# Moving tile loads and stores from ScalarE's queue to GpSimd's in an attention and expert kernel

## The chip, the cores and the metric

The kernel runs on one core of a Trainium2 chip. A core has five engines, each with its own instruction stream that it works off in order: TensorE (PE in the profile; PEld is its weight load), VectorE (DVE), ScalarE (ACT), GpSimd (POOL) and SyncE (SP). An engine that reaches an instruction whose input isn't there waits, and all that stands behind it waits too. Transfers between memory and the core's buffers are carried by 16 DMA engines, but an instruction on one of the engines' streams starts each of them. The metric is the device time of one launch in microseconds; the time before is the median of three runs, 1396.2 us (1394.3 to 1397.18).

## What is computed

The input is x of shape (8, 1024, 256), float32: 8192 rows of 256. The output adds two branches to x, both fed with the layer norm of x:

```
xn  = (x - mean) / sqrt(var + 1e-5)
out = x + attention(xn) + experts(xn)

# attention: 16 heads of 16, causal, linear
q, k = elu(xn Wq^T) + 1, elu(xn Wk^T) + 1;   v = xn Wv^T
kv, ks = cumsum over rows of (k outer v), of k
attention = (q . kv / max(q . ks, 1e-6)) Wo^T

# experts: 8 experts, the two best of each row
logits = xn Wr + br;  two largest, softmax over the two -> weights c
experts = sum over the two of c_e * (silu(xn W1_e) * (xn W3_e)) W2_e
```

W1 and W3 are 256 x 512 per expert, W2 is 512 x 256. Which rows go to which expert is known only while the kernel runs.

## The kernel before

**Tiles.** The rows are cut into 16 tiles of 512 rows (index t, four chunks of 128). A tile's raw rows are `xb`. Four steps make it ready: `moments(t, n)` finds mean and variance (L272) and, for tiles after the fifth, the inverse square root by Newton steps on VectorE (L281 to L291), and writes the factors of the normalisation into the table `tab` (L294 is the last step); `normalise(t)` scales the rows, on ScalarE from tile 4 on (L307); `turn(t)` transposes them on TensorE (L322), copies the result `xnT` out on ScalarE (L327) and stores it to memory as `xnT_d[t]` (L331), from where attention reads it much later; `logits_turned(t)` and `add_logits` compute the router's logits (L340, L345, L361, L351). Every four tiles `route` finds the two best experts of their rows and counts the rows per expert (`both` L413, `run` L421, `cnt_ps` L427 on TensorE).

**Experts.** The rows chosen for an expert are put together in expert tiles of 128 rows (index j), 135 at most. The first 25 come from the first four tiles of x, whose routing is done at the start, in `first_batch()`; the rest are listed when all 16 tiles are routed. For expert tile j: `ffn_load` has GpSimd gather the rows `xg` (L1085) and their `entry` (L1090: weight and the two factors of the norm); `ffn_weights` reads the expert's number `te_i` (L1112) on SyncE and starts the two loads of its W1 and W3 (L1122, 512 KB each); `ffn_norm` scales the rows (L1097, ScalarE); `ffn_turn` transposes them (L1106, copy L1108); `ffn_hidden` makes the gate and up products (`gu_ps` L1139, silu L1147, `hT` L1150); `ffn_out` the second product (`y_ps` L1158) and `y` (L1165, VectorE); `ffn_store` has GpSimd scatter-add y to memory (L1169), for the first 25 into `acc_d`, later into the output.

**The loops.** A start section, whose order is written out by hand, readies tiles 0 to 4, routes 0 to 3 and lists the first 25 expert tiles. Then SyncE issues the loads of W2, tile 6, the copy of x into `acc_d` and the store of the table (L1060), which the entries are gathered from. The main loop (L1208 on) runs over j. In each of its first eleven steps after j = 0 it also readies tile t = 4 + j: every second step the moments of two tiles, then normalise, turn, and the load of tile t + 5 into one of five buffers, then logits and every fourth tile the routing. At j = 0 the loads of tiles 7, 8 and 9 are issued. Interleaved with this the attention of the tiles goes on in small steps, among them two `reciprocal` instructions of 128x512 per tile (L843, their input `den` L842), the masked scores (`s_sb` L872) and the add of the result to memory from GpSimd (L936, L938). `ffn_step(j)` gathers for j + 3, loads weights for j + 2, turns j + 1 and finishes j − 1.

**What sets the order.** Outside the start section the order of the instructions on each engine is not the order of the source: a planner chooses it when the program is built, from priorities and costs of its own; `in_order` and `issue_after` hold some of it. A change in the source can therefore change the order on engines that it doesn't touch. [...]

## Time and profile before

| | |
|---|---|
| median of the three runs | 1396.2 us (1394.3 to 1397.18) |
| profiled execution | 1388.92 us; its span is 1387.1 us, 1.8 us lie around it |
| granted TensorE clock | 0.99 |
| TensorE | 1328.5 us busy, 96% of the span |
| VectorE, ScalarE, GpSimd | 52%, 35%, 38% |
| loads of xb on ScalarE's queue | 9 of 512 KB, 6.0 us from issue to landing (median) |
| stores of xnT on ScalarE's queue | 15 of 512 KB, 4.7 us |
| main loop from the first expert product (53.4 us) to the last prepared tile (about 165 us) | 111.6 us, TensorE 106.5 us busy |

The profile is of one execution, 7.3 us under the median of the runs, so a sum from its rows is a difference to be added to the median. The columns of a timeline row are its start and duration in microseconds, the engine (a q behind it marks the engine's DMA issue), the line of the kernel, the operation, output and inputs with their sizes, how many instructions are taken together, and in brackets the engine's idle time before it and what ended that. A row of waits names the waiting engine and line, what it waited for, and the sum, number and longest of the waits in us. A row of DMA issues gives the issuing queue, number, size and time from issue to landing in us. A busy share is an average; in the tile loop the shares differ from those of the whole.

### The profile page before, as it was taken

How to read it: one execution, taken by the hardware profiler on the slowest of the kernel's cores; microseconds unless marked ns; L12 is line 12 of the kernel's file. 1: busy time of each engine (PE TensorE's matmuls, PEld its weight loads, DVE VectorE, ACT ScalarE, POOL GpSimd, SP SyncE). 2: the span in 40 equal slices, each digit the busy share in tenths (PEclk: the TensorE clock that was granted, in tenths of full speed). 3: DMA queues.
4: the chain of work that ended last, by engine and by line, in shares of the span. 5: the costliest groups of instructions: out<-in, count | busy, mean ns of one | idle time of the engine just before them, and what ended most of it. 6: DMA issues, size and time to landing. Idle time of an engine off the chain costs nothing.

```text
span 1387.1 us, 27907 instructions
## 1 busy us (share of the span) xinstructions
PE 1328.5 (96%) x10906; PEld 1127.2 (81%) x10906; DVE 728.0 (52%) x1428; ACT 488.7 (35%) x914; POOL 528.3 (38%) x457
## 2 busy tenths in 40 slices
PE   5799999999999999999999999999999999999996
PEld 4578887878888888888888888888788788888895
DVE  7786589784353536354453536363544435363631
ACT  5466351141514233252525142342524151423321
POOL 3533332223334333434433333443434244334432
PEclk9999999999999999999999999999999999999999
DMA  9687653455756555555656555565647375555553
GB/s 346 236 275 234 180 169 109 120 143 145 211 160 152 164 124 145 150 145 151 152 147 164 147 151 152 140 173 139 162 129 175 109 173 160 132 164 138 147 151 80
DMA packets 129412, 223.56 MB, mean 161 GB/s; under 512 B 14818, under 2 KB 53346, under 8 KB 128994
## 3 DMA queue, kind: packets, MB, share of 16 engines
q1 hardware_dynamic: 84306, 165.95, 36.9%
q0 software_dynamic: 38064, 43.22, 19.3%
q10 hardware_dynamic: 6912, 12.58, 2.5%
q8 instruction: 90, 1.47, 0.4%
q14 instruction: 40, 0.33, 0.1%
HBM read 187.91 MB, written 44.29 MB: 167 GB/s over the span
## 4 chain that ended last, share of the span: by engine, by line
PE 82%; DVE 11%; ACT 3%; issue 2%; DMA 2%; POOL 0%; POOLq 0%; ACTq 0%; DVEq 0%
PE gu_ps L1139 32%; PE y_ps L1158 15%; PE s_ps L865 6%; PE o_ps L906 4%; PE a_ps L928 4%; PE zq L764 4%; PE zkk L780 3%; PE zkv L780 3%; PE kv_ps L880 2%; DVE rden L843 2%; PE xg_t L1106 2%; PE held_ps L696 2%; PE o_ps L899 2%; PE den L842 2%; DVE ksum L832 2%
## 5 line engine op out<-in xcount | busy, mean ns | idle before, releaser
L1139 PEld LDWEIGHTS gu_ps<-xgT,w 128*128 128x128 f32 x4224 | 494.7, 193 | 28.8 <-issue 17.2
L1139 PE MATMUL gu_ps<-xgT,w 128*128 128x128 f32 x4224 | 511.6, 278 | 2.3 <-DVE s_sb L872 1.9
L1085 POOL DMA_INDIRECT xg<-in_x_dram,src_i x132 | 129.8, 983 | 547.7 <-ACT xgT L1108 437.8
L1158 PE MATMUL y_ps<-w_sb,hT 128*128 x1056 | 251.9, 380 | 2.5 <-DVE hT L1150 1.3
L1169 POOL DMA_INDIRECT out_dram<-y,dst_i x107 | 173.6, 1622 | 159.4 <-DVE y L1165 85.1
L1150 DVE TENSOR_TENSOR hT<-gu_ps,hT 128x512 f32<-128x512 f32 x132 | 90.4, 685 | 248.2 <-PE gu_ps L1139 229.2
L1147 ACT ACTIVATE hT<-gu_ps 128x512 f32<-128x512 f32 x132 | 78.8, 597 | 381.1 <-PE gu_ps L1139 380.2
L1158 PEld LDWEIGHTS y_ps<-w_sb,hT 128*128 128x128 f32 x1056 | 190.0, 190 | 25.9 <-issue 2.6
L872 DVE TENSOR_TENSOR s_sb<-s_ps,causal 128x512 f32<-128x512 f32 x256 | 163.2, 683 | 73.6 <-PE s_ps L865 71.8
L1165 DVE TENSOR_SCALAR y<-y_ps,entry 128x256 f32<-128x256 f32 x132 | 63.7, 482 | 137.6 <-PE y_ps L1158 137.6
L1090 POOL DMA_INDIRECT entry<-tab_d,of_i x107 | 111.2, 1040 | 37.8 <-issue 31.7
L865 PE MATMUL s_ps<-qm,kT 32*128 32x256 f32 x1024 | 107.6, 412 | 3.4 <-DVE rden L843 2.0
L843 DVE RECIPROCAL rden<-den 128x512 f32<-128x512 f32 x32 | 105.4, 3329 | 3.4 <-PE den L842 3.4
L1108 ACT COPY xgT<-xg_t 128x256 f32<-128x256 f32 x132 | 49.0, 372 | 152.3 <-PE xg_t L1106 150.7
L865 PEld LDWEIGHTS s_ps<-qm,kT 32*128 32x128 f32 x1024 | 61.6, 185 | 39.1 <-issue 19.5
L933 ACT COPY at<-a_ps 128x256 f32<-128x256 f32 x64 | 23.8, 372 | 176.9 <-PE a_ps L928 176.7
L1097 ACT ACTIVATE xg<-xg,entry 128x256 f32<-128x256 f32 x132 | 79.6, 603 | 5.6 <-issue 5.6
L928 PE MATMUL a_ps<-wo_sb,oT 128*128 128x256 f32 x256 | 67.2, 384 | 5.7 <-DVE oT L914 5.6
L906 PE MATMUL o_ps<-s_sb,va 128*32 128x128 f32 x2048 | 71.8, 278 | 0.0
L764 PE MATMUL zq<-xnT,wq_sb 128*128 128x512 f32 x128 | 61.0, 609 | 0.0
L928 PEld LDWEIGHTS a_ps<-wo_sb,oT 128*128 128x128 f32 x256 | 47.0, 190 | 16.6 <-DVE oT L914 9.4
L1169 POOL DMA_INDIRECT acc_d<-y,src_i x25 | 44.0, 1761 | 42.2 <-DVE y L1165 30.7
(199 smaller groups left out, 1440.6 us busy)
## 6 DMA issues: line engine op xcount, KB each, us to landing
w<-in_w_dram SPq DMA_DIRECT2D x264, 512.0 KB, 4.4
xnT_d<-xnT ACTq DMA_DIRECT2D x15, 512.0 KB, 4.7
xnT<-xnT_d SPq DMA_DIRECT2D x15, 512.0 KB, 5.9
out_dram<-in_x_dram SPq DMA_DIRECT2D x12, 512.0 KB, 5.2
out_dram<-at POOLq DMA_DIRECT2D x12, 512.0 KB, 7.7
xb<-in_x_dram ACTq DMA_DIRECT2D x9, 512.0 KB, 6.0
w_sb<-in_w_dram SPq DMA_DIRECT2D x4, 1024.0 KB, 11.8
xb<-in_x_dram SPq DMA_DIRECT2D x7, 512.0 KB, 7.4
```

The source lines that it names most:

```text
L764: nc.tensor.matmul(z, lhsT=wq_sb[:, k, bass.ts(o, P)], rhs=xnTs[t][:, k, :], start=(k == 0), stop=(k == KC - 1),)
L843: nc.vector.reciprocal(rden[:, o, :], den)
L865: nc.tensor.matmul(s_ps[r][:, hh].rearrange("p a l -> p (a l)"), lhsT=kT[rows, hh, span], rhs=qm[rows, hh, :, span], start=True, stop=True,)
L872: nc.vector.tensor_tensor(sm, s_ps[r].rearrange("p k a l -> p (k a) l"), causal_b, ALU.mult)
L906: nc.tensor.matmul(o_ps[32 * r : 32 * r + 32, hh, :], lhsT=va[:, c, 4 * hh + r, a, :], rhs=s_sb[r][:, 2 * hh + a, :], start=(first and a = ...
L928: nc.tensor.matmul(a_ps, lhsT=oT[:, hh, :], rhs=wo_sb[:, hh, :], start=(hh == 0), stop=(hh == 1),)
L1085: nc.gpsimd.indirect_dma_start(out=xg[j], out_offset=None, in_=x_rows[:, :], in_offset=bass.IndirectOffsetOnAxis(ap=src_i[:, i : i + 1], a ...
L1090: nc.gpsimd.indirect_dma_start(out=entry[j], out_offset=None, in_=table[:, :], in_offset=bass.IndirectOffsetOnAxis(ap=num_i[:, i : i + 1], ...
L1139: done = nc.tensor.matmul(ps[:, i, :], lhsT=w13[:, k, bass.ts(i, P)], rhs=xgT[j][:, k, :], start=(k == 0), stop=(k == KC - 1),)
L1150: nc.vector.tensor_tensor(hT, gu[1], hT, ALU.mult)
L1158: done = nc.tensor.matmul(y_ps, lhsT=hT[:, i, :], rhs=w2_sb[:, bass.ds(e * (IC * H) + i * H, H)], start=(i == 0), stop=(i == IC - 1),)
L1169: nc.gpsimd.indirect_dma_start(out=rows[:, :], out_offset=bass.IndirectOffsetOnAxis(ap=dst_i[:, i : i + 1], axis=0), in_=ys.pop(j), in_off ...
```

## The change

Three edits:

1. `turn` issues the stores of `xnT_d[t]` for t = 5 to 15 on GpSimd; those of tiles 1 to 4 stay on ScalarE.
2. The loads of `xb` in the main loop (tiles 7, 8 and 9 at j = 0, tiles 10 to 15 one per step) are issued on GpSimd. Together 20 DMAs change their queue. The data, the buffers and the sizes are the same.
3. In `first_batch` the count of experts per place (`numbers_of`: one reduction and one cast on VectorE, 0.33 and 0.20 us) stands right behind `past`, which it reads, and no longer among the steps that build the list. `te_i` is therefore ready earlier on VectorE; SyncE's first weight loads and TensorE's reads of W2 use it.

```diff
@@ turn
-            last_store[0] = nc.scalar.dma_start(out=xnT_d[t], in_=xnT.rearrange("p k l -> p (k l)"))
+            queue = nc.scalar if t <= FB else nc.gpsimd
+            last_store[0] = queue.dma_start(out=xnT_d[t], in_=xnT.rearrange("p k l -> p (k l)"))
@@ first_batch
         past = past_experts(upto, N1, e_one, "past")
+        _, te_i = numbers_of(past, N1, "1")
         taken = f_one.tile([P, E], F32, name="taken")
...
-                if j == 0 and a == 2 * PART:
-                    _, te_i = numbers_of(past, N1, "1")
@@ main loop
         if j == 0:
             for i in range(3, 6):
-                load_x(t + i, nc.scalar)
+                load_x(t + i, nc.gpsimd)
...
             if t + 5 < NBLK:
-                load_x(t + 5, nc.scalar)
+                load_x(t + 5, nc.gpsimd)
```

The order that the planner gives the new program differs from the old one as follows. On GpSimd the instructions per tile stand as scatter of y, gather of entry, store of xnT, load of xb, gather of xg. On VectorE the statistics (L272) of tile 7 stand before the last Newton steps of tile 5; both reciprocals (L843) before L294 of tiles 6 and 7; the statistics of tile 11 before the routing chain of tiles 4 to 7 and before y of j = 2; those of tile 13 before y of j = 3, of tile 14 before y of j = 4, of tile 15 before y of j = 5. On TensorE the products of j = 1 and 2 stand before the transposes of tile 6, and `cnt_ps` of tiles 4 to 7 stands before the products of j = 4. On SyncE the first weight load stands before the store of the table. From about 300 us of the old execution on, TensorE's order is the same.

## The prediction

> **What bounds the kernel now.** I read the page first, then stretches of the tile loop, then each engine's waits and its timeline. The page, busy time and the chain that ended last:

> ```profile
> PE 1328.5 (96%) x10906; PEld 1127.2 (81%) x10906; DVE 728.0 (52%) x1428; ACT 488.7 (35%) x914; POOL 528.3 (38%) x457
> PE 82%; DVE 11%; ACT 3%; issue 2%; DMA 2%; POOL 0%; POOLq 0%; ACTq 0%; DVEq 0%
> ```

> TensorE (PE) is the bound as a whole. The edited lines act only between 35 and 165 us, so stretches (columns: PE, PEld, DVE, ACT, POOL busy with counts, clock, DMA share, GB/s):

> ```profile
> 35.00:70.00 35.00, 26.13 (x201) 18.94 (x201) 28.02 (x119) 15.73 (x32) 19.43 (x19) 0.95 0.70 235
> 70.00:105.00 35.00, 33.13 (x286) 27.82 (x285) 29.51 (x110) 21.88 (x44) 13.24 (x11) 1.00 0.88 270
> 105.00:140.00 35.00, 34.59 (x323) 29.61 (x322) 20.87 (x77) 22.71 (x46) 14.17 (x12) 1.00 0.79 239
> 165.00:1387.00 1222.00, 1189.98 (x9725) 1016.36 (x9723) 611.58 (x989) 402.20 (x741) 458.05 (x370) 0.99 0.56 148
> ```

> From 70 us on PE is 95 to 99% busy: nothing that only relieves ACT (22 of 35 us) can pay there, while an idle microsecond forced on PE is not won back later, because the last stretch has 97% PE and, as the changed program's order shows, the same PE order from about 300 us on. DVE is the second engine (29.5 of 35 us), and it works in order. Its waits in this stretch on the loads in question:

> ```profile
> DVE st L272 <- DMA xb<-in_x_dram: 4.6, 3, 1.9
> ```

> So three loads of x already come a little late, by 1.9 us at most: there is no slack in them. That is the row on which this case turns.

> **The change, part by part.** The program of the changed kernel can be laid beside the old one instruction by instruction; orders below are from that, times from the old trace.

> *1. Issue taken off ACT.* Eleven stores and nine loads leave ACT: 11 x 0.34 + 8 x 0.45 + 1 x 1.43 (rows below) = 8.8 us. ACT had 13 us idle in 70–105, and PE's waits there end on DVE or on order, so it is worth 0: PE's own queue and DVE hide it. If that cover were gone it would be about 1 us per tile at the places where a norm of xg is late; I keep −1 as an end.

> *2. Issue put on POOL.* The same 20 cost POOL more:

> ```profile
> 73.27 0.34 ACTq L331 DMA_DIRECT2D xnT_d<-xnT  x1
> 73.65 1.43 ACTq L145 DMA_DIRECT2D xb<-in_x_dram  x1
> 80.88 0.45 ACTq L145 DMA_DIRECT2D xb<-in_x_dram  x1
> ...
> 73.04 1.60 POOL L1169 DMA_INDIRECT acc_d<-y,src_i  x1 [4.53 <-DVE y L1165]
> 74.95 0.99 POOL L1090 DMA_INDIRECT entry<-tab_d,num_i  x1 [0.30 <-issue]
> 77.90 0.96 POOL L1085 DMA_INDIRECT xg<-in_x_dram,src_i  x1 [1.96 <-ACT xgT L1108]
> 186.63 1.41 POOL L938 DMA_DIRECT2D acc_d<-at  x1 [2.78 <-ACT at L933]
> ```

> A plain 512 KB DMA on POOL is 1.41 us, a smaller one (L936 on the page of groups) 1.03. Per expert tile POOL has 1.60 + 0.99 + 0.96 = 3.55 us, and gets 1.41 + 1.03 to 1.41 more plus 0.3 between each: about 7.5 us of a cycle of 9. It isn't full. What matters is that POOL is in order. The order per tile becomes: scatter of y (waits for DVE's y), entry gather, store of xnT (waits for ACT's copy), load of xb, gather of xg. So the load of tile t+5 now stands behind a scatter that waits for DVE, and in DVE's new order that y stands behind the BatchNorm statistics of the *previous* loaded tile. Load → statistics → y → scatter → next load: a loop, which the old kernel had not, since ACT issued each load without y.

> *3. First experts counted earlier.* DVE does 0.33 + 0.20 us of the same work, sooner: 0. SP's first weights no longer wait for it:

> ```profile
> 39.97 18.78 SPq L1122 DMA_DIRECT2D w<-in_w_dram  x7
> ...
> 50.95 0.60 ACT L1097 ACTIVATE xg<-xg,entry 128x256 f32<-128x256 f32 x1 [5.63 <-issue]
> 51.61 0.44 PE L1106 MATMUL xg_t<-ident,xg 128*128 128x128 f32 x2 [4.39 <-ACT xg L1097]
> ```

> They start at about 34.7 instead of 39.97, the first five land ahead of the first entry gather (6.35 us from issue to landing here, 4.1 in the median) and give it up to 2 us back. PE waits 4.39 us at that place. But now the statistics of tile 7 precede the last Newton steps of tile 5, and its load comes on POOL after the third pair of gathers (51.2 + at least 5, then 3.9 of DVE work): I keep 1.0 of the 2.0. Ends: −2 and 0; the table store, now behind a weight load on SP, can take 0.5 away.

> *4. DVE's order.* Rows of DVE and ACT at tile 6:

> ```profile
> 68.38 3.35 DVE L843 RECIPROCAL rden<-den 128x512 f32<-128x512 f32 x1
> 72.67 3.35 DVE L843 RECIPROCAL rden<-den 128x512 f32<-128x512 f32 x1
> ...
> 66.37 0.60 ACT L307 ACTIVATE xb<-xb,tab 128x256 f32<-128x256 f32 x1 [3.44 <-DVE tab L294]
> ```

> Both reciprocals now stand before the last step (L294) of tiles 6 and 7; before, after it. Tile 6 then has its factors at about 75.8, is normalised at 76.5, and PE, which reaches its transposes at 72.5, waits 4.0 us; some of it was idle anyway, so the next xg transpose is 79.9 for 76.75: +3.1, with the 1.0 of part 3, +2.1. Ends: 0, if the reciprocals run earlier because den (PE) does, and 5.

> *5. The loop.* The copy of tile 6 ends at 78.55, the store takes 1.3, so xb11's load is issued at 80.1 (73.65 before). Let L be the time from issue to landing of such a load on POOL. The six ACT loads of 60–112 took 7.85, 7.14, 5.80, 5.33, 6.56 and 5.91 from the start of issue, mean 6.4; with 1.41 in place of 0.45 of issue this is 7.4; the page's row for a 512 KB DMA on POOL is 7.7:

> ```profile
> out_dram<-at POOLq DMA_DIRECT2D x12, 512.0 KB, 7.7
> ```

> I take 7, as the later four are nearer (5.9 + 1.0 = 6.9). Ends: 5, the shortest on ACT, and 9, when POOL's issue stretches. By the new orders, xb11 lands at 80.1 + L. Then y of tile j = 2 comes 6.7 us later (statistics of xb11, and the routing chain between them), and POOL has 4.8 to do (1.6 + 0.3 scatter, 1.3 entry, 1.3 to 1.6 store) before xb13 is issued, which lands at 91.6 + 2L. From there 5.2 to y of j = 3 and 4.8 to xb14: 101.6 + 3L. From there 1.3 and 4.8 to xb15: 107.7 + 4L = 135.7. The old kernel began xb15's statistics at 115.27, after a wait of 1.21 us that PE did not feel. PE's loss is so 4L − 7.6 − 1.2 = 4L − 8.8, which holds parts 3 and 4 already: 19.2 at L = 7, 11.2 at 5, 22.0 at 7.7, 27.2 at 9. On the way the count of tiles 4 to 7 (L427), now ahead of the gate products of j = 4 on PE, costs 5.5 us at 90, and the logits of tile 11 come at 142 for 123.

> After xb15 no load is left and the stores alone (1.03 to 1.41, no reader soon) wait for nothing late. PE goes on 19 us late to the end.

> **Sum.** 0 (ACT) + 19.2 (loop, with −1.0 and +3.1 in it) on the profiled execution: span 1387.1 and 1.8 around it, 1388.9, gives 1408. That execution is 7.3 us under the median of 1396.2, so the median is predicted at 1396.2 + 19 = **1415**.

> [...] The trace shows POOL's DMA instructions stretched where DVE works beside them:

> ```profile
> 177.29 2.37 POOL L1085 DMA_INDIRECT xg<-in_x_dram,src_i  x1 [10.55 <-PE xg_t L1106]
> 210.68 3.98 POOL L1169 DMA_INDIRECT acc_d<-y,src_i  x1 [3.55 <-DVE y L1165]
> ```

> They are 0.96 and 1.60 elsewhere. [...] The trace shows it in few rows of the stretch before 165, so I leave it to the upper end.

> [...]

> **Rivals.**
> (a) *Not slower.* POOL issues the loads before DVE asks, as y comes early enough, and what is left is part 3 (−1 to −2), ACT's −1 and up to 1.9 of DVE's waits, since xb7 is issued at 51.2 instead of 53.75: −1 to −5, 1391 to 1395. For it: POOL is busy in 13 of 35 us only. Against: loads came late by up to 1.9 us when issued 6 us earlier. It decides if DVE's waits on xb stay under about 5 us in all.
> (b) *The order alone.* Part 4 without the loop, as den and y run ahead: +2 to +5, 1398 to 1401. It needs L near 4 (only one ACT load was that quick, 4.06, before 60 us).
> (c) *Stretched issue.* L of 8.5 to 9 by the rows of the stretched DMAs: +25 to +28, 1421 to 1424. For it: DVE is 84% busy in 70–105; against: POOL's rows there are 0.95 to 1.61.
> (d) *Nothing changes*: transfers hidden, parts 3 and 4 cancel: 1394 to 1399.

> **How the numbers follow.** 0.2% (2.8 us) is about what a measurement of this kernel tells from no change. Loop with L of 5 to 8: 0.57; (c) 0.14; (b) 0.10; (d) 0.05; (a) 0.14, of which 0.10 gain over 0.2%. The forecast is 1415. Range 1397 to 1427: its low end takes in (b) and half of (d), its top is (c) and 3 us of the spread of the medians; outside lie (a), half of (d), and some 0.04 above. The likeliest case's own range is 1407 to 1419. Faster 0.10 (of a), same 0.09 (0.04 of a, 0.04 of d, 0.01 of b), slower 0.81.

> **What would show it.** In the profile after: DVE's waits on xb (L272) grow from 4.6 to 20 us or more, the xb loads show on POOL's queue with 6 to 8 us to landing; PE's busy time in 70–140 falls by about 15 to 20 us; PE waits for the counts' operands (L427 on DVE) and for tile 6's transposes (on ACT's L307); the first xg norm starts before 50.95; from 300 us on stretches as before, shifted. POOL's own rows at 1.4 and 1.0 us. The forecast is wrong if xb loads are issued on POOL before about 74, 81 and 88, if y comes ahead of the statistics in time, or if PE finds enough other work ahead of each wait.

## The result, and the profile after

The changed kernel took 1415.06 us in the median of four runs (1411.48 to 1417.42), the kernel before 1396.56 in four (the three given above and one more); the ratio is 1.0132, with a 95% interval of 1.011 to 1.0154. That is 18.5 us slower, 1.3%. The prediction was 1415 us, range 1397 to 1427, slower with a chance of 0.81. So the number was right; whether it was right for its reasons is what the rest is about.

The profiled execution has a span of 1409.7 us. Its busy totals are nearly those of before, GpSimd's excepted, which has 20 instructions and 12 us more:

```profile
PE 1334.1 (95%) x10906; PEld 1128.9 (80%) x10906; DVE 727.8 (52%) x1428; ACT 489.0 (35%) x914; POOL 540.4 (38%) x477
```

The same stretches as before (PE, PEld, DVE, ACT, POOL busy with counts, clock, DMA share, GB/s):

```profile
35.00:70.00 35.00, 26.05 (x203) 19.07 (x202) 27.17 (x101) 14.27 (x28) 21.66 (x24) 0.95 0.75 251
70.00:105.00 35.00, 26.89 (x208) 21.34 (x207) 23.02 (x98) 17.73 (x35) 14.15 (x14) 0.85 0.67 203
105.00:140.00 35.00, 30.27 (x267) 25.21 (x267) 19.93 (x86) 19.08 (x42) 14.37 (x14) 0.90 0.61 174
140.00:175.00 35.00, 34.19 (x314) 28.72 (x312) 13.25 (x37) 14.69 (x29) 15.65 (x15) 1.00 0.69 208
```

Between 70 and 140 us TensorE is busy 57.2 us, where it was 67.7, and has executed 475 products, where it had 609. Its granted clock there is 0.85 and 0.90, where it was 1.00: TensorE both stood and ran slower. From 140 to 175 us it is full again. VectorE's waits for loads of x in 40 to 200 us, and TensorE's longest wait in 50 to 330:

```profile
DVE st L272 <- DMA xb<-in_x_dram: 17.1, 5, 5.6
```

```profile
PE cnt_ps L428 <- DVE sq L289: 5.8, 1, 5.8
```

The 4.6 us have become 17.1. How VectorE's waits become TensorE's is read from three timelines, mainly at 84 to 106 us (GpSimd's, VectorE's, TensorE's):

```profile
84.16 1.02 POOL L1090 DMA_INDIRECT entry<-tab_d,num_i  x1 [0.30 <-issue]
85.15 0.61 POOL L332 DMA_DIRECT2D xnT_d<-xnT  x1
85.73 0.85 POOL L145 DMA_DIRECT2D xb<-in_x_dram  x1
...
89.70 0.16 DVE L291 SCALAR_TENSOR_TENSOR y<-sq,bits 128x8 f32<-128x8 f32 x1
94.98 0.43 DVE L272 BATCH_NORM_STATS2 st<-xb 128x6 f32<-128x256 f32 x1 [5.12 <-DMA xb<-in_x_dram]
95.33 0.27 DVE L398 TENSOR_TENSOR hits<-desc,first 128x128 f32<-128x128 f32 x1
95.69 0.34 DVE L414 TENSOR_TENSOR both<-hits 128x128 f32<-128x128 f32 x1
...
89.61 0.71 PE L865 MATMUL s_ps<-qm,kT 32*128 32x256 f32 x6
96.08 0.80 PE L428 MATMUL cnt_ps<-both,upto_neg 128*128 128x128 f32 x2 [5.76 <-DVE sq L289]
102.25 4.09 PE L1139 MATMUL gu_ps<-xgT,w 128*128 128x128 f32 x32
```

Tile 12's load is issued at 85.73 and landed by 94.98. VectorE reaches its statistics at 89.86 and stands. The two routing instructions behind it (`hits`, `both`) need 0.6 us and no load, but stand too; TensorE's count of tiles 4 to 7 needs `both`, and the products of expert tile 4 stand behind the count. (The row of waits names `sq`, which ended within 0.1 us of `both`; the count reads `both`.) Tile 12's load was late twice over: it was issued 4.9 us later than before (80.88), and it took 9.2 us to land where it took 5.8. The second part came back in every version with this load on GpSimd (8.6 to 9.3 us); what makes it was not tested. The same chain is there with tile 14: its load is issued at 112.73, VectorE waits 5.58 us for it until 120.32, y of expert tile 4 stands behind its statistics, a router transpose on TensorE waits 2.95 us, and y's scatter on GpSimd waits 6.30 us, with the load of tile 15 behind it (issued at 125.25):

```profile
112.73 0.85 POOL L145 DMA_DIRECT2D xb<-in_x_dram  x1
120.32 0.75 DVE L272 BATCH_NORM_STATS2 st<-xb 128x6 f32<-128x256 f32 x2 [5.58 <-DMA xb<-in_x_dram]
120.99 0.47 DVE L1165 TENSOR_SCALAR y<-y_ps,entry 128x256 f32<-128x256 f32 x1
121.60 0.44 PE L362 MATMUL lg_t<-ident,lgT 128*128 128x128 f32 x1 [2.95 <-DVE y L1165]
121.74 1.64 POOL L1169 DMA_INDIRECT acc_d<-y,src_i  x1 [6.30 <-DVE y L1165]
125.25 0.83 POOL L145 DMA_DIRECT2D xb<-in_x_dram  x1
```

To follow the loss I use one mark: the start of the silu (ScalarE) of each expert tile, against the same mark before. In the changed kernel it comes 3.9 us earlier for tile 0, 2.4 later for tile 3, 10.6 for tile 4, 15.7 for tile 7, and 16.9 for tiles 14 to 18. So the loss stands complete at about 180 us. The mark of tile 16, before and after:

```profile
237.72 0.60 ACT L1147 ACTIVATE hT<-gu_ps 128x512 f32<-128x512 f32 x1 [12.98 <-PE gu_ps L1139]
254.60 0.60 ACT L1147 ACTIVATE hT<-gu_ps 128x512 f32<-128x512 f32 x1 [12.98 <-PE gu_ps L1139]
```

### The profile page after: what moved, and what is told of

Read it like the earlier page. It is cut to its first block, busy times and chain, and to the rows that moved or that the text cites. A ratio compares the mean times of both kernels' runs of the same rounds, so it can differ in the third digit from the quotient of the medians.

```text
span 1409.7 us, 27929 instructions
## 1 busy us (share of the span) xinstructions
PE 1334.1 (95%) x10906; PEld 1128.9 (80%) x10906; DVE 727.8 (52%) x1428; ACT 489.0 (35%) x914; POOL 540.4 (38%) x477
## 3 DMA queue, kind: packets, MB, share of 16 engines
q0 software_dynamic: 40944, 53.71, 21.6%
## 4 chain that ended last, share of the span: by engine, by line
PE 81%; DVE 11%; ACT 3%; issue 2%; DMA 2%; POOL 1%; another core or an unknown queue 0%; POOLq 0%; DVEq 0%; ACTq 0%
PE gu_ps L1139 31%; PE y_ps L1158 14%; PE s_ps L865 6%; PE o_ps L906 5%; PE a_ps L928 4%; PE zq L764 4%; PE zkk L780 3%; PE zkv L780 3%; PE kv_ps L880 2%; DVE rden L843 2%; PE xg_t L1106 2%; PE held_ps L696 2%; PE o_ps L899 2%; PE den L842 2%; DVE ksum L832 1%
## 5 line engine op out<-in xcount | busy, mean ns | idle before, releaser
L1085 POOL DMA_INDIRECT xg<-in_x_dram,src_i x132 | 129.5, 981 | 542.2 <-ACT xgT L1108 431.0
L1169 POOL DMA_INDIRECT out_dram<-y,dst_i x107 | 173.4, 1621 | 160.1 <-DVE y L1165 85.9
L872 DVE TENSOR_TENSOR s_sb<-s_ps,causal 128x512 f32<-128x512 f32 x256 | 163.5, 684 | 78.9 <-PE s_ps L865 51.6
L1165 DVE TENSOR_SCALAR y<-y_ps,entry 128x256 f32<-128x256 f32 x132 | 63.5, 481 | 138.0 <-PE y_ps L1158 101.0
L1090 POOL DMA_INDIRECT entry<-tab_d,of_i x107 | 111.4, 1041 | 32.6 <-issue 31.7
L843 DVE RECIPROCAL rden<-den 128x512 f32<-128x512 f32 x32 | 105.4, 3329 | 4.0 <-PE den L842 4.0
L1108 ACT COPY xgT<-xg_t 128x256 f32<-128x256 f32 x132 | 49.0, 372 | 148.0 <-PE xg_t L1106 146.3
L933 ACT COPY at<-a_ps 128x256 f32<-128x256 f32 x64 | 23.8, 372 | 185.8 <-PE a_ps L928 185.6
L1097 ACT ACTIVATE xg<-xg,entry 128x256 f32<-128x256 f32 x132 | 79.6, 603 | 2.8 <-DVE v L275 2.8
L1169 POOL DMA_INDIRECT acc_d<-y,src_i x25 | 43.7, 1750 | 49.2 <-DVE y L1165 36.7
## 6 DMA issues: line engine op xcount, KB each, us to landing
w<-in_w_dram SPq DMA_DIRECT2D x264, 512.0 KB
xnT<-xnT_d SPq DMA_DIRECT2D x15, 512.0 KB
out_dram<-in_x_dram SPq DMA_DIRECT2D x12, 512.0 KB
out_dram<-at POOLq DMA_DIRECT2D x12, 512.0 KB
xnT_d<-xnT POOLq DMA_DIRECT2D x11, 512.0 KB
xb<-in_x_dram POOLq DMA_DIRECT2D x9, 512.0 KB
xb<-in_x_dram SPq DMA_DIRECT2D x7, 512.0 KB
```

The lines of the kernel that those rows point to most:

```text
L843: nc.vector.reciprocal(rden[:, o, :], den)
L872: nc.vector.tensor_tensor(sm, s_ps[r].rearrange("p k a l -> p (k a) l"), causal_b, ALU.mult)
L1085: nc.gpsimd.indirect_dma_start(out=xg[j], out_offset=None, in_=x_rows[:, :], in_offset=bass.IndirectOffsetOnAxis(ap=src_i[:, i : i + 1], a ...
L1090: nc.gpsimd.indirect_dma_start(out=entry[j], out_offset=None, in_=table[:, :], in_offset=bass.IndirectOffsetOnAxis(ap=num_i[:, i : i + 1], ...
L1169: nc.gpsimd.indirect_dma_start(out=rows[:, :], out_offset=bass.IndirectOffsetOnAxis(ap=dst_i[:, i : i + 1], axis=0), in_=ys.pop(j), in_off ...
```

## The experiments

Two numbers help to compare them: the mark for expert tile 16 in the profiled execution, less 237.72 us of before ("delay at tile 16"), and TensorE's busy time between 50 and 176 us times the missing share of its clock, summed over slices of 1 us ("clock loss"). Both are of one execution each. Ratios are against the kernel before on the same chip.

| | ratio (95%) | delay at tile 16, us | clock loss, us |
|---|---|---|---|
| before | 1 | 0 | 1.7 |
| changed | 1.0132 (1.011 to 1.0154) | +16.9 | 7.6 |
| early count alone | 0.9996 (0.9978 to 1.0014) | −2.1 | 1.7 |
| queues alone | 1.0133 (1.0107 to 1.0159) | +16.6 | 10.0 |
| changed, scatter behind the next load | 1.0075 (1.0051 to 1.0099) | +8.0 | 3.8 |
| changed, late statistics | 1.0021 (1.0009 to 1.0034) | +1.6 | 1.6 |
| early count, late statistics, ScalarE's queue | 1.0015 (0.9998 to 1.0032) | −0.9 | 1.6 |
| changed, products in the wait | 1.0181 (1.0159 to 1.0202) | +22.3 | 10.1 |
| loads alone | 1.0100 (1.0077 to 1.0123) | +14.6 | 8.4 |
| stores alone | 1.0004 (0.999 to 1.0017) | +4.2 | 8.4 |
| stores alone, products in the wait | 1.0048 (1.0031 to 1.0066) | +6.0 | 1.6 |
| early count, products in its waits | 1.0019 (0.9999 to 1.0038) | +2.1 | 2.0 |

Theory: the loss is a loop. Load of x on GpSimd → statistics on VectorE → y and routing behind them → scatter of y on GpSimd → next load. Rivals: the order alone (both reciprocals ahead of tile 6's factors); GpSimd's issue or slow transfers as such; the two parts of the change acting on each other.

**1. The early count alone.**

```diff
 # changed kernel, with all loads and stores back on ScalarE
-            queue = nc.scalar if t <= FB else nc.gpsimd
+            queue = nc.scalar
...
-                load_x(t + i, nc.gpsimd)
+                load_x(t + i, nc.scalar)
...
-                load_x(t + 5, nc.gpsimd)
+                load_x(t + 5, nc.scalar)
```

> Only the earlier count of the first experts; all 20 DMAs stay on ScalarE, and the order of VectorE and GpSimd in the tile loop is that of the kernel before. In the changed kernel the first transpose of gathered rows on TensorE was at 48.7 us instead of 51.6. If the early weights are a gain that the loop then covered up: 2 to 3 us faster than before (about 1393.5 to 1394.5). If the gain is eaten by what is late next (the table, tile 5's factors): within 1 us of before. If the early count is itself a part of the loss: slower.

Measured: 0.9996, and in the trace −2.1 us that stay. The start is as expected: the first transpose of gathered rows comes at 48.70 instead of 51.61. A gain of 2 us lies within the interval (−3.1 to +1.9 us), so the runs don't show it to be one; the traces of one execution each show 2.1. A part of the loss it is not.

**2. The queues alone.**

```diff
 # changed kernel, with the count back in its old place
         past = past_experts(upto, N1, e_one, "past")
-        _, te_i = numbers_of(past, N1, "1")
...
+                if j == 0 and a == 2 * PART:
+                    _, te_i = numbers_of(past, N1, "1")
```

> The 20 DMAs on GpSimd without the earlier count. VectorE's and GpSimd's orders in the tile loop are those of the changed kernel. Loop theory: slower than before by 17 to 22 us (the whole loss of 18.5 plus the 2 to 3 that the early count gives): 1414 to 1418. If the two parts act on each other (the early weights collide with the loads): clearly less, 1400 to 1410.

Measured: 1.0133, +18.5 us. The 20 DMAs carry the whole loss, and the early count gives nothing back beside them (16.6 and 16.9 us): it makes expert tile 0 come 3.5 us earlier than here, and by tile 3 nothing of that is left.

**3. The loop cut on GpSimd.**

```diff
     def load_x(t, queue):
         xbs[t] = f_x.tile([P, NCH, H], F32, tag="xb", name=f"xb{t}")
-        in_order(queue.dma_start(out=xbs[t], in_=xf[t]))
+        last_load[0] = queue.dma_start(out=xbs[t], in_=xf[t])
+        in_order(last_load[0])
...
             if stored[0] < j - behind:
-                ffn_store(stored[0])
+                if j < LISTS:
+                    with tc.issue_after(last_load[0].ins):
+                        ffn_store(stored[0])
+                else:
+                    ffn_store(stored[0])
                 stored[0] += 1
...
-        ffn_step(j, LATE if N1 < j <= N1 + LATE else 0)
+        ffn_step(j, LATE if N1 < j <= N1 + LATE else 1 if j <= LISTS else 0)
```

> The changed kernel with one edge moved: on GpSimd the scatter of y of expert tile j stands behind the load of the next tile of x, so no load of x waits for y; VectorE's order is unchanged. In the changed kernel the loads of tiles 12 to 15 came behind scatters that cost 2 to 7 us each with their waits. Loop theory in full (the load waits for y): most of the loss goes, 1398 to 1405. Rival, order on VectorE (statistics ahead of routing and y, any late load stalls it) with a late issue for other reasons: the loss stays at 10 or more, 1407 to 1415.

Measured: 1.0075, +10.4 us (7.1 to 13.7): between the two expectations. Every instruction of VectorE and TensorE between 50 and 165 us keeps its order; only the scatters have moved. The loads no longer wait for y (GpSimd, tiles 13 to 15 in this run):

```profile
89.03 0.82 POOL L147 DMA_DIRECT2D xb<-in_x_dram  x1
...
107.23 0.81 POOL L147 DMA_DIRECT2D xb<-in_x_dram  x1
...
116.32 0.82 POOL L147 DMA_DIRECT2D xb<-in_x_dram  x1
```

They were at 93.40, 112.73 and 125.25. But tile 12's load (81.91) still holds up the routing: TensorE still waits 4.7 us for the count:

```profile
92.14 0.79 PE L431 MATMUL cnt_ps<-both,upto_neg 128*128 128x128 f32 x2 [4.74 <-DVE sq L292]
```

So the edge from y to the next load is worth about 8 of the 18 us; the other 10 come without it.

**4. The loop cut on VectorE.**

```diff
-                with tc.issue_after(last_token[0].ins):
+                with tc.issue_after((made[j - 4] if j > 5 else last_token[0]).ins):
                     for _ in moments(t, 2):
                         pass
...
-        nc.vector.tensor_scalar(ys[j], y_ps, entry.pop(j)[:, 0:1], None, ALU.mult)
+        made[j] = nc.vector.tensor_scalar(ys[j], y_ps, entry.pop(j)[:, 0:1], None, ALU.mult)
```

> The changed kernel with GpSimd's order untouched, but the statistics of tiles 10 to 15 are held behind y of expert tiles 2, 4 and 6 on VectorE, so that y and the routing of tiles 4 to 7 no longer wait for a load. Loop theory: the loop is cut on its other side, VectorE's waits on loads of x fall from 17 us to under 4, and the time is within 4 us of before: 1393 to 1400. Rival, GpSimd's issue or its slow transfers as such are the price: 1408 to 1416 still. Rival, the order alone (both reciprocals ahead of tile 6's factors): 1399 to 1402.

Measured: 1.0021, +2.9 us (1.2 to 4.7). GpSimd's order is untouched, the two reciprocals still stand ahead of tile 6's factors, and tile 12's load is issued at 84.28 instead of 85.73, tile 13's at 91.87 instead of 93.40: no better in relation to the rest. But nothing that TensorE needs stands behind them. VectorE waits for loads of x 1.0 us in all, and TensorE's count waits for nothing but its own input, 0.2 us:

```profile
DVE st L272 <- DMA xb<-in_x_dram: 1.0, 1, 1.0
87.20 1.04 PE L322 MATMUL tp<-ident,xb 128*128 128x128 f32 x8
88.41 0.49 PE L428 MATMUL cnt_ps<-both,upto_neg 128*128 128x128 f32 x2 [0.17 <-DVE both L414]
```

The loop theory holds, with its weight on VectorE: the price is the statistics' place ahead of routing and y, once the load comes late. What is left, 2.9 us, is the net of GpSimd's issue, tile 6's late factors and whatever the early count gains.

**5. Late statistics without GpSimd.**

```diff
 # the early count alone, and on top the edit of experiment 4
+                with tc.issue_after((made[j - 4] if j > 5 else last_token[0]).ins):
```

> The early count kept, all 20 DMAs on ScalarE as before, and the statistics of tiles 10 to 15 held behind y of expert tiles 2, 4 and 6. VectorE then waits for no load of x after 80 us. If the loop's other half (late loads of x) cost the kernel before something too: 2 to 5 us faster than before. If the 3.9 to 4.6 us of such waits there were hidden from TensorE: within 2.5 us of before, as the early count alone.

Measured: 1.0015, +2.1 us with an interval that reaches from −0.3 to +4.4. VectorE's waits on loads of x, 3.9 us with the early count alone, are gone from its list, and nothing is gained: with ScalarE's queue these waits were hidden from TensorE. This run also prices the queue by itself: it differs from experiment 4 only in the queue of the 20 DMAs and in what the planner made of that, and their ratios, 1.0015 and 1.0021, each against before on its own chip, lie 0.8 us apart, within either interval.

**6. Products of constants in the changed kernel's long wait**, to see whether the lowered clock follows the idle time.

```diff
         cnt_ps = ps_y.tile([P, E * n + E], F32, tag="y", name="cnt_ps")
+        if a == ROUND:
+            with tc.issue_after(last_turn[0].ins):
+                for _ in range(20):
+                    nc.tensor.matmul(cnt_ps[:, 0:P], lhsT=ones, rhs=ident, start=True, stop=True)
         for m, what in ((upto_neg, both), (ones, run)):
 # last_turn: the last transpose of turn(t); the routing of tiles 4 to 7 is traced behind turn(8)
```

> The changed kernel with 20 matrix products of constants put on TensorE ahead of the count of tiles 4 to 7, where it stood idle for 5.8 us; their result is overwritten. They take about 4.3 to 5.6 us, so they fit the idle time. The changed kernel's granted clock was 0.77, 0.50 and 0.70 in the three 5 us slices from 90 us on. If the idle time is what lowers the clock: the clock stays at 1.0 in 90 to 105 and the loss shrinks by 2 to 5 us, 1.009 to 1.011 times before. If the clock falls for another reason, or does not matter: 1.013 as the changed kernel, or worse by the products.

Measured: 1.0181. The products filled 90.0 to 94.7 and the clock was 1.00 there, but the count still waited 1.95 us, then a router transpose 2.61 us, and the clock was 0.50 from 98 to 108.2 us. The edit only moved the wait; it settles nothing on the clock.

**7 and 8. The loads alone, the stores alone** (with the early count).

```diff
 # loads alone                                   # stores alone: this line as changed, and
-            queue = nc.scalar if t <= FB else nc.gpsimd
+            queue = nc.scalar                     # load_x(..., nc.scalar) in both places
```

> Only the nine loads of x on GpSimd (and the early count); the stores of the transposed tiles stay on ScalarE. The loads still stand behind scatters of y, and statistics of tiles 11 to 13 before y and routing. Loop theory: most of the loss is here, 8 to 16 us slower than before; the store's place in the queue (0.6 us and its wait for ScalarE's copy) is the smaller part.

> Only the eleven stores on GpSimd (and the early count); the loads of x stay on ScalarE, where nothing waits for y. No loop is left. Loop theory: within 3 us of before, 1385 to 1391 on the chip of the last runs. Rival, GpSimd's queue as such (its gathers and scatters behind stores that wait for ScalarE): 5 us or more slower.

Measured: 1.0100 for the loads, +13.9 us, and 1.0004 for the stores. The loads' VectorE waits are 21.6 us, the stores' 3.1. Most of the loss is the loads', as expected. The two don't add up to the whole (14.5 of 18.5 us), and they are not pure parts of it: without the stores the planner puts each load straight behind the scatter of y, ahead of the gather of `entry`. The stores alone leave a puzzle: no difference in the runs, but +4.2 us at tile 16 of the profiled execution where the early count alone has −2.1. TensorE's idle time in 50 to 176 us is 5.4 us there, less than the 6.6 of the early count alone. The profiled execution was the slowest of the ten (1392.17 us, 4.0 over their median), and in it the clock accounts for the difference: 8.4 us of clock loss for 1.7 (stores alone, stretches, then two rows of TensorE):

```profile
80.00:86.00 6.00, 6.00 (x49) 5.31 (x47) 4.22 (x23) 2.73 (x5) 1.94 (x3) 1.00 0.93 305
86.00:88.00 2.00, 0.17 (x1) 0.00 (x0) 2.00 (x13) 1.29 (x3) 1.30 (x1) 1.00 1.01 395
88.00:99.00 11.00, 10.39 (x53) 8.26 (x54) 8.11 (x31) 5.58 (x10) 2.11 (x3) 0.54 0.40 121
...
88.61 0.59 PE L428 MATMUL cnt_ps<-both,upto_neg 128*128 128x128 f32 x2 [2.44 <-DVE den L453]
94.76 5.81 PE L1139 MATMUL gu_ps<-xgT,w 128*128 128x128 f32 x32
```

TensorE stands for 2.4 us at the count, and for the next 11 us it runs at 0.54 of its clock: its 32 gate products take 5.81 us at 94.76, where they take 3.73 at full clock (the changed kernel, at 70.03).

**9. The stores alone, with products in that wait.**

```diff
 # on top of the stores alone; the routing is traced behind turn(8), as in 6
+        if a == ROUND:
+            with tc.issue_after(last_turn[0].ins):
+                for _ in range(14):
+                    nc.tensor.matmul(cnt_ps[:, 0:P], lhsT=ones, rhs=ident, start=True, stop=True)
```

> Only the stores on GpSimd, as in the run of the stores alone, with 14 matrix products of constants (about 0.23 us each, 3.3 us) ahead of the count of tiles 4 to 7 on TensorE; their result is overwritten. In the run of the stores alone TensorE waited 2.4 us there, and from 88.6 to 99 us the granted clock was 0.50, so that the 32 gate products behind took 5.8 us instead of 3.7. Five score products (1.1 us) come behind the count now. If idle time lowers the clock: no half clock in 86 to 99, and expert tile 10 comes at +1 or less against the kernel before in its trace, where the stores alone had +4.1. If the clock falls for another reason: half clock again, +5.

The stretch in question:

```profile
80.00:89.00 9.00, 9.00 (x76) 7.90 (x75) 8.17 (x38) 4.68 (x11) 5.07 (x5) 1.00 0.89 236
89.00:93.00 4.00, 4.00 (x38) 4.00 (x37) 3.86 (x21) 3.54 (x6) 2.48 (x2) 1.00 1.04 410
93.00:105.00 12.00, 10.62 (x97) 9.14 (x96) 10.23 (x40) 6.33 (x13) 1.93 (x3) 1.00 0.62 188
```

```profile
89.66 3.29 PE L432 MATMUL cnt_ps<-ident,ones 128*128 128x128 f32 x28
98.07 3.84 PE L1145 MATMUL gu_ps<-xgT,w 128*128 128x128 f32 x32 [1.38 <-DVE s_sb L878]
```

With the wait filled, the clock stays at 1.00 and the gate products take 3.84 us instead of 5.81. From expert tile 2 to 10 this run loses 3.6 us against before (+2.4 to +6.0), the stores alone lost 6.5 (−2.3 to +4.1). So here the idle time is what lowers the clock, as far as one execution of each can tell. The delay at tile 16 was expected at +1 and is +6.0, and the time is 1.0048, for something else: ScalarE stood 5.7 us behind its table load at 52 us, in front of the first silu, and TensorE 8.3 us with it. Experiment 10 has this too and no other run; its cause is not settled, and the times of these two runs are not used.

**10. The early count, with products in its own waits.**

```diff
-        for _ in range(3):
+        for _ in range(4):
             idle_ps = ps_mm.tile([P, TB], F32, tag="mm", name="idle_ps")
...
+            if t == FB + 1 and k == 0:
+                for _ in range(5):
+                    nc.tensor.matmul(tp[:, 0:P], lhsT=ones, rhs=ident, start=True, stop=True)
```

> The early count alone (all 20 DMAs on ScalarE), with a fourth product of constants behind the three that stand ahead of the first gathered rows (0.9 us of the 1.55 us idle there), and five small ones (1.2 us) ahead of the transposes of tile 5, where TensorE waited 1.16 us; the half clock stood at 58.9 to 62.3 us in the run of the early count alone. If idle time lowers the clock: no half clock there, 1.5 to 2 us less than the early count alone in the trace at expert tile 10 (−3.6 to −4.1 against the kernel before), a ratio of about 0.997 to 0.998. If not: −2 or worse, since the products themselves may delay the transposes.

Measured: 1.0019, +2.1 at tile 16. ScalarE's stand of 8.6 us at 53.6 covers whatever it could show: inconclusive. No version beat the kernel before by more than the runs can tell; the early count alone comes nearest.

## Why the prediction was right

**Parts 1 and 2 (issue).** ACT's relief was priced at 0: the stores alone (1.0004) and the early count alone (0.9996) bear it out. POOL's issues were priced too high: 0.85 us for a load instead of 1.41, 0.60 for a store instead of 1.03, with no gap ahead. The row of 1.41 is not of a plain DMA: L938 adds to what is in memory (`accum_op` in the kernel). As said, their cost is not where the loss is.

**Part 3 (early count).** Predicted −2 at the first rows, −1.0 net. Measured −2.9 and, at the transposes of tile 5, −1.1 (58.92 for 60.02). Its size in the whole, −2.1 in the trace when alone, is lost again beside the queues.

**Part 4 (order).** Tile 6's factors came at 74.4 instead of the predicted 75.8, the next transpose of gathered rows at 78.45 instead of 76.75: +1.7 for +2.1. Right.

**Part 5 (the loop).** The mechanism is the one named, and the forks agree: cutting it on VectorE leaves 2.9 of 18.5 us, cutting it on GpSimd 10.4. What the prediction put together as one loop is two things of about equal weight: a late load that holds up routing at 90 us, which needs no scatter waiting ahead of it, and the edge from y to the next load. One turn of the loop was not there. The prediction had tile 13's load hold up y of expert tile 3; VectorE came to that tile's statistics at about 104.9 and did not wait for its load. y of tile 3 came late because the gate products stood behind the count, thus behind tile 12's load, and ran after a stretch at half clock:

```profile
104.86 0.42 DVE L272 BATCH_NORM_STATS2 st<-xb 128x6 f32<-128x256 f32 x1
106.61 0.68 DVE L1150 TENSOR_TENSOR hT<-gu_ps,hT 128x512 f32<-128x512 f32 x1
108.44 0.48 DVE L1165 TENSOR_SCALAR y<-y_ps,entry 128x256 f32<-128x256 f32 x1
```

The sizes, in order: L was taken as 7 and the loads that VectorE waited for took 5.2 (tile 11), 9.2 (tile 12), 7.6 (tile 14) and 5.1 us (tile 15) up to the first statistics, 6.8 in the mean. The wait for the count at 90 us was 5.8 (predicted 5.5). Tile 11's load landed at 84.1 (predicted 87.1), tile 14's at 120.3 (122.6), tile 15's at 130.3 (135.7): the chain ran 2 to 5 us ahead of the reckoning.

**The term that failed.** 4L − 8.8 was to give 19.2 us from the loop alone, holding parts 3 and 4. The delay was 16.9, and 5.9 of it is clock loss (7.6 less the 1.7 of before), which no step of the prediction has: it passed stalls on one for one. The rest is TensorE's idle time in 50 to 176 us, 18.2 for 7.2: 11.0 us, which by the formula would be L of 5. So the loop was oversized by about 8 us, and a second price of stalls, the clock at 0.50 from 92.7 to 103 and from 120 to 126.9 us, was left out. The two errors nearly cancel; the predicted number is better than its working. (The 5.9 is worked out from the slices and is no run of its own. The split is not fixed either: with the queues alone the same delay is 8.2 us of idle time and 8.3 of clock.) Two of the prediction's signs fell short accordingly: VectorE's waits were 17.1 us for "20 or more", and TensorE's busy time in 70 to 140 fell by 10.6 for "15 to 20", as products at half clock count as busy for longer (32 gate products took 5.81 us at 0.54 with the stores alone, 3.73 at full clock).

**The end.** "PE goes on 19 us late" holds in kind: the delay is 16.9 at the mark of tile 16 and 19.5 at that of tile 126. In between it moves: before's profiled execution ran at 0.50 from 311.9 to 318.7 us, where the changed kernel's was at 1.00 from 126.9 to 340, and the delay of tile 24 is 14.2. So the difference of the two spans, 22.6, is less telling than that of the medians, 18.5.

**The rivals.** (a) falls: the loads alone lose 13.9 us. (b), the order alone, stays in place in experiment 4 and so is within the 2.9 us that this leaves, its own size, but it is not what happened; its condition, L near 4, was not right either, since 4L − 8.8 is 7.2 there. (c) falls as it was put: L was 6.8 in the mean, and the loads' issue was never stretched between 50 and 130 us (0.77 to 0.85 us). But the one load that held up the count took 9.2, the size that (c) had, without a longer issue. (d) falls with the time. The stretched rows of before, which set the upper end, have no counterpart in the issue of these loads; the scatter of 3.98 us that before has at 210.68, behind the tile loop, is there with 3.99 us at 227.57. The mean of the transfers is near on the two queues (6.8 us on GpSimd's, 6.4 on ScalarE's) and is no guide to the time of this change, since the place in the queue was the price.

## What to carry to other kernels

Ask of each load that moves to another queue two things: what stands ahead of it there and waits, and what stands behind its first reader on the reader's engine. The second was the larger part here: holding the readers of the late loads behind the work that TensorE waited for took back 15.6 of 18.5 us with the loads left where they were. Where a planner sets the order, an edit of queues is an edit of the order on engines that it doesn't name, so compare the orders before the times.

## What the runs showed of the hardware

```profile
88.00:92.00 4.00, 2.32 (x18) 1.62 (x16) 1.86 (x11) 2.50 (x5) 2.18 (x3) 1.00 0.99 371
92.00:96.00 4.00, 0.00 (x0) 0.00 (x0) 1.01 (x7) 0.00 (x0) 2.23 (x3) 0.59 1.08 353
96.00:103.00 7.00, 6.92 (x41) 4.95 (x42) 4.96 (x24) 1.55 (x2) 0.00 (x0) 0.50 0.31 119
103.00:118.00 15.00, 15.00 (x137) 13.04 (x136) 8.59 (x40) 12.41 (x27) 6.09 (x6) 1.00 0.62 174
```

The length of the low stretch, added up from slices of 1 us, is 3.4 us in the kernel before (52.5 to 55.9), 3.4, 10.2 and 6.8 in the changed kernel and 6.8 and 10.2 with the stores alone: one, two or three times 3.4. In these runs the length of a pause does not decide by itself. Pauses of 2.1 us (experiment 3, at 126.9) and 2.2 us (experiment 6, at 141.2) passed at 1.00. With the early count alone the clock fell at 58.9 us with no pause over 1.2 us in the 10 us ahead, and in the kernel before at 311.9 with TensorE busy for 3.40 of the 3.50 us ahead, mostly on score products of 32 rows. The low stretches of the changed kernel start at 58.61, 92.74 and 120.05 us, 34.13 and 27.31 us apart, which is 10 and 8 times 3.413; so where a pause falls in this beat may decide, but no run varied it.

Pauses of 2.4 us (stores alone) and 2.9 us (changed kernel) were enough here, and the low stretch of 10.2 us with the stores alone went on while TensorE was busy nearly all the time (10.39 of the 11 us shown above). What pause is short enough these runs don't settle.
